# The sums of a layer norm as accumulating passes of ScalarE, and a state copy moved to GpSimd, in the first stage of a four-layer kernel

## Chip, cores and metric

One core of one Trainium2 chip. The metric is the device time of one execution in microseconds (us), on that core. All runs quoted here are of the fast state; "before" is timed again on the same chip in every set of runs, and its medians lie between 10865.7 and 10869.8 us.

The engines are named as the profile does: PE (TensorE matmul), PEld (its weight loads), DVE (VectorE), ACT (ScalarE), POOL (GpSimd), SP (the queue that issues the loads).

## The reference, cut to what matters

The model is four layers. The change touches only the first: a layer norm and two selective recurrences ("mambas") over 4 x 4096 tokens, one on the normed channels and one on the flipped ones, and a residual sum.

```python
def _layernorm(x, g, b):
    mu = jnp.mean(x, axis=-1, keepdims=True)
    var = jnp.mean(jnp.square(x - mu), axis=-1, keepdims=True)
    return (x - mu) * jax.lax.rsqrt(var + LN_EPS) * g + b
...
xs = _layernorm(x.reshape(b, -1, c), ln_g, ln_b)        # c = 192
y1 = _mamba(xs, ...)                                     # in_proj, conv, silu, x_proj, softplus,
y2 = _mamba(jnp.flip(xs, axis=-1), ...)                  # then h = dA * h + dBx, y = C . h
out = xs + y1 + y2
```

## The kernel before

It works through 32 units of 512 tokens. A unit has two recurrences of 12 quads each; a quad is four scans of 128 rows x 512 tokens on DVE, so a unit is 96 scans, 48 for each recurrence. A quad in program order:

```python
def product(self, u, k):       # DVE, or POOL for every fourth quad ("h_apart"): h = dtx * B
    engine.tensor_tensor(h, u["rows", k // 2, 1], B..., ALU.mult)
def decay(self, u, k, j):      # ACT: dA = exp(dt * A) into one of three PSUM buffers
    self.nc.scalar.activation(dA, u["rows", k // 2, 0][:, j, :], AF.Exp, scale=self.A[...])
def step(self, u, k, j):       # DVE: h = scan(dA, h), starting from the saved state
    self.nc.vector.tensor_tensor_scan(h[:, j, :], dA, h[:, j, :], self.state[...], ALU.mult, ALU.add)
def read(self, u, k):
    nc, h = self.nc, u["h", k]
    if self.shared:            # only in the first stage
        nc.scalar.copy(self.state[:, k, :], h[:, :, T - 1])
    else:
        nc.gpsimd.tensor_copy(self.state[:, k, :], h[:, :, T - 1])
    nc.gpsimd.tensor_tensor(h, h, u["C", k % 2]..., ALU.mult)   # in place, so after the copy
# sum: PE adds h up into y, which DVE then multiplies by z (the "gate", m_y in the traces);
# spread: PE writes B (PSUM), C and Bs, once per recurrence and parity of k
```

Behind these scans, all other work is dripped into the engines' queues step by step ("one step" is one scan): the norm of the next unit, its two fronts, and the output. Each is a generator; `Piece(wait=n)` holds the next piece back for n steps. The order is fixed when the program is built, and the traces here show each of DVE, ACT and POOL working through its own queue in that order (in a timeline below, ACT's dA stands behind a copy that waits 5.79 us).

```python
def front(self, xn, first, u):
    def project(e, to):
        ps = behind.bank([128, T], "ps_in")
        ...                                                      # PE: two matmuls
        return behind.later(lambda: nc.scalar.copy(to, ps))      # ACT, some steps later
    made = []
    for d in range(ND):
        yield Piece(1.7, bank=True)
        made.append(project(d, raw[:, d, K - 1 :]))              # "raw": the first projections
    ...                  # convolution, Silu, x_proj, Softplus, stores, then the same for z

def norm(u):
    ...
    for q in range(nq):                                          # nq = 4
        if q == 2:
            yield Piece(wait=1)
        nc.vector.bn_stats(stats[:, q, :], xt[:, q, :])
        nc.vector.bn_aggr(mv[:, q, :], stats[:, q, :])
    yield Piece(wait=1)
    ...                                                          # four small POOL operations: rs, shift
    yield Piece(wait=3)
    for q in range(nq):
        nc.scalar.activation(xs[:, q, :], xt[:, q, :], AF.Identity, scale=rs[...], bias=shift[...])
    ...                                                          # PE transposes, ACT copies: xT
# in the main loop, per unit:
    last = [units[n - 1]["added"]] if n else []
    behind.add(3, norm(following), Piece(wait=3, after=last))
    behind.add(1, front(following, i), Piece(after=[following["normed"]]))
```

## Time and profile before

| | before |
|---|---|
| time, median of 3 | 10868.96 us |
| first stage | about 90 to 5340 us of the span |
| one unit | 163.9 us (mean distance of the loads of x, 30 units) |
| DVE busy, 900 to 4900 us | 3891 of 4000 us |
| POOL / PE / ACT busy there | 3533 / 3287 / 2717 us |
| DVE's waits for dA, 100 to 5200 us | 62.5 + 40.0 = 102.5 us |

A busy share says how full an engine is. A bracket at the end of a timeline row says how long the engine sat idle ahead of it and who ended that. A wait is charged to the last releaser only; to see why that one was late, one has to follow it back through its own queue. This case turns on that.

### The profile page before, as it was taken

Reading aid. Unit: us, or ns where it says so; the run is one execution under the profiler, and the core shown is the slowest. Engines: PE = TensorE matmul, PEld = TensorE weight load, DVE = VectorE, ACT = ScalarE, POOL = GpSimd, SP = SyncE. Lnnn points to the kernel's source line nnn. Section 1 sums busy time; section 2 is a strip of 40 time slices with the busy share of each in tenths; the row PEclk is TensorE's granted clock in tenths of the full one; section 3 lists DMA queues with packets and bytes.
Section 4 is the critical chain, followed back from the end, with each engine's and each line's share of the span. In section 5 each row is a group of like instructions: output and inputs, shape, how many; then the busy total and the mean of one; then the engine's idle time right before and its main releaser. Section 6 shows DMA issues by size and latency. Waiting matters only on the chain. (4 is left out here: it accounts for less than half of the span.)

```text
span 10866.7 us, 97590 instructions
## 1 busy us (share of the span) xinstructions
PE 9179.8 (84%) x31352; PEld 3644.1 (34%) x31352; DVE 9098.4 (84%) x7962; ACT 6566.6 (60%) x9784; POOL 7032.3 (65%) x2688
## 2 busy tenths in 40 slices
PE   6888878888887887887679999999999987889898
PEld 2222222222322222222223333333333333455555
DVE  7999999999999999999698888888888885555552
ACT  5666666666666666666466666656666663444443
POOL 5888888888888888888666656656656661111100
PEclk7777777777777777777678889889889887999999
DMA  5666666666666666666454545445444443122110
GB/s 158 177 181 180 177 177 183 175 176 182 177 177 179 177 178 179 176 178 180 128 151 135 140 127 143 133 125 141 129 134 133 133 121 82 41 50 64 42 40 18
DMA packets 969560, 1515.13 MB, mean 139 GB/s; under 512 B 244346, under 2 KB 277150, under 8 KB 968534
## 3 DMA queue, kind: packets, MB, share of 16 engines
q1 hardware_dynamic: 968190, 1505.85, 51.4%
q8 instruction: 247, 4.05, 0.2%
q10 hardware_dynamic: 856, 3.05, 0.1%
q14 instruction: 267, 2.19, 0.1%
HBM read 1295.45 MB, written 213.12 MB: 139 GB/s over the span
## 5 line engine op out<-in xcount | busy, mean ns | idle before, releaser
L574 DVE TENSOR_TENSOR_SCAN h<-dA,m_state,h 128x512 f32<-128x512 f32 x3840 | 4668.9, 1266 | 487.4 <-ACT dA L568 422.7
L590 POOL TENSOR_TENSOR h<-h,C 128x2048 f32<-128x2048 f32 x960 | 4345.4, 4531 | 621.6 <-ACT m_state L587 480.7
L568 ACT ACTIVATE dA<-dtE,m_A 128x512 f32<-128x512 f32 x4608 | 3106.1, 687 | 1332.9 <-DVE h L574 1227.8
L561 DVE TENSOR_TENSOR h<-dtxE,B 128x2048 f32<-128x2048 f32 x960 | 2170.6, 2261 | 78.6 <-DMA dtxE<-r_dtx 65.9
L599 PE MATMUL y<-h,gather 128*32 128x512 f32 x7680 | 1281.3, 746 | 422.9 <-POOL h L590 345.2
L452 PE MATMUL ps_in<-xT,m_in_w 96*128 96x512 f32 x1536 | 939.5, 759 | 258.6 <-ACT raw L455 127.1
L1300 POOL TENSOR_TENSOR d<-d,rs 128x512 f32<-128x512 f32 x64 | 86.8, 1357 | 1589.7 <-DVE rs L1299 1569.1
L470 PE MATMUL ps_conv<-raw,m_conv 128*128 128x512 f32 x2112 | 989.3, 617 | 1.7 <-ACT xc L475 1.7
L574 DVE TENSOR_TENSOR_SCAN h_apart<-dA,m_state,h_apart 128x512 f32<-128x512 f32 x768 | 922.3, 1260 | 40.0 <-ACT dA L568 40.0
L590 POOL TENSOR_TENSOR h_apart<-h_apart,C 128x2048 f32<-128x2048 f32 x192 | 870.2, 4532 | 39.7 <-ACT m_state L587 38.0
L561 POOL TENSOR_TENSOR h_apart<-dtxE,Bs 128x2048 f32<-128x2048 f32 x192 | 889.6, 4633 | 6.0 <-ACT Bs L550 6.0
L452 PEld LDWEIGHTS ps_in<-xT,m_in_w 96*128 96x128 f32 x1536 | 351.3, 241 | 827.2 <-issue 420.5
L589 POOL COPY m_state<-h 128x4 f32<-128x4 f32 x384 | 72.3, 188 | 849.5 <-DVE h L574 813.5
L470 PEld LDWEIGHTS ps_conv<-raw,m_conv 128*128 128x128 f32 x2112 | 417.9, 202 | 599.0 <-issue 562.4
L1049 PE MATMUL ps_dw<-strip,dw 96*96 96x512 f32 x1152 | 578.7, 650 | 1.3 <-ACT x L1058 0.9
L599 PEld LDWEIGHTS y<-h,gather 128*32 128x32 f32 x7680 | 164.7, 117 | 1225.4 <-POOL h L590 552.0
L506 POOL TENSOR_TENSOR raw<-dt,xc 128x1536 f32<-128x1536 f32 x96 | 330.0, 3437 | 294.6 <-ACT dt L505 294.6
L486 PE MATMUL ps_x<-xc,m_pack 128*44 128x512 f32 x576 | 351.0, 758 | 199.5 <-ACT xc L482 194.6
L1465 PE MATMUL sed_ps<-xn,sed 64*128 64x256 f32 (+3 forms) x2944 | 485.9, 404 | 7.0 <-DVE y L1484 7.0
L568 ACT ACT_TABLE_LOAD x345 | 442.6, 1283 | 28.5 <-DMA dtE<-r_dt 22.3
L452 PE MATMUL ps_in<-xn,m_in_w 96*128 96x512 f32 x768 | 399.0, 666 | 47.4 <-ACT z L455 31.2
L378 PE MATMUL ps_o<-hid,t 128*96 128x512 f32 x768 | 390.4, 647 | 34.3 <-ACT hid L371 13.0
(193 smaller groups left out, 12217.1 us busy)
## 6 DMA issues: line engine op xcount, KB each, us to landing
dtE<-r_dt SPq DMA_DIRECT2D x2304, 256.0 KB, 5.0
dtxE<-r_dtx SPq DMA_DIRECT2D x2304, 256.0 KB, 4.1
r_dt<-dt SPq DMA_DIRECT2D x96, 768.0 KB, 4.0
r_dtx<-raw SPq DMA_DIRECT2D x96, 768.0 KB, 5.4
x<-x SPq DMA_DIRECT2D x64, 384.0 KB, 3.9
img<-x SPq DMA_DIRECT2D x28, 512.0 KB, 8.2
xt<-in_x SPq DMA_DIRECT2D x32, 384.0 KB, 5.8
x<-o SPq DMA_DIRECT2D x32, 384.0 KB, 5.0
```

What stands on the lines that cost most here:

```text
L378: nc.tensor.matmul(ps, self.w2[:, m, bass.ts(k, CP)], h[:, m, :], start=(m == 0), stop=(m == NH - 1),)
L452: nc.tensor.matmul(ps, self.in_w[:, k, bass.ts(e, 128)], xn[:, k, :], start=(k == 0), stop=(k == 1))
L470: nc.tensor.matmul(ps, self.conv[:, d, j, :], raw[:, d, j : j + T], start=(j == 0), stop=(j == K - 1))
L486: nc.tensor.matmul(ps, self.x_w[:, d, :], xc[:, d, :], start=(d == 0), stop=(d == ND - 1))
L506: nc.gpsimd.tensor_tensor(dtx, dt, xc, ALU.mult)
L561: engine.tensor_tensor(h, u["rows", k // 2, 1], u[B, k % 2].unsqueeze(1).broadcast_to([128, 4, T]), ALU.mult)
L568: self.nc.scalar.activation(dA, u["rows", k // 2, 0][:, j, :], AF.Exp, scale=self.A[:, k, j : j + 1])
L574: self.nc.vector.tensor_tensor_scan(h[:, j, :], u.pop(("dA", k, j)), h[:, j, :], self.state[:, k, j : j + 1], ALU.mult, ALU.add,)
L590: nc.gpsimd.tensor_tensor(h, h, u["C", k % 2].unsqueeze(1).broadcast_to([128, 4, T]), ALU.mult)
L599: self.nc.tensor.matmul(u["ys"][32 * j : 32 * j + 32, :], self.ex.gather[:, i // 2, :], h[:, j, :], start=(i == 0), stop=(i == 3 and not s ...
L1049: nc.tensor.matmul(ps, dw[:, k, j, :], s[:, k, dy : dy + rows, dx : dx + HW], start=(j == 0), stop=(j == 8),)
L1465: nc.tensor.matmul(out, sed[p, int(h is not None), i ^ position(k, s), cols], xn[b, g][p, c, :], start=group(t) not in begun, stop=left[gr ...
```

## The change

The intent: DVE is the fullest engine of the stage, so take the norm's statistics off it. ACT makes the two sums in passes with an accumulator output, and loses the state copies, which POOL does itself ahead of its product.

```diff
     def read(self, u, k):
-        if self.shared:
-            nc.scalar.copy(self.state[:, k, :], h[:, :, T - 1])
-        else:
-            nc.gpsimd.tensor_copy(self.state[:, k, :], h[:, :, T - 1])
+        nc.gpsimd.tensor_copy(self.state[:, k, :], h[:, :, T - 1])
 ...
         def norm(u):
-            for q in range(nq):
-                if q == 2:
-                    yield Piece(wait=1)
-                nc.vector.bn_stats(stats[:, q, :], xt[:, q, :])
-                nc.vector.bn_aggr(mv[:, q, :], stats[:, q, :])
-            yield Piece(wait=1)
-            (POOL: rs = (var + EPS) ** -0.5; shift = -mean * rs)
+            def sums(func, to, **args):
+                for q in range(nq):
+                    if q:
+                        yield Piece(wait=1)
+                    nc.scalar.activation(xs[:, q, :], xt[:, q, :], func, accum_out=to[:, q : q + 1], ...)
+            yield from sums(AF.Identity, shift)
+            yield Piece(wait=2)
+            nc.gpsimd.tensor_scalar(shift, shift, -1.0 / C, None, ALU.mult)
+            yield Piece(wait=2)
+            yield from sums(AF.Square, rs, bias=shift)
+            yield Piece(wait=2)
+            (POOL: rs = (rs / C + EPS) ** -0.5; shift = shift * rs)
             yield Piece(wait=3)
             (the last pass, unchanged)
```

The chain of the norm gets longer: in the built order its last transposed copy moves from scan 33 of a unit to scan 43.

More of the change, by code (lines that the diff above doesn't have):

```diff
@@ L776, in norm @@
             xt = u["x"]
-            stats = work.tile([128, nq, 6], F32, name="stats")
-            mv = work.tile([128, nq, 2], F32, name="mv")
-            rs = work.tile([128, nq], F32, name="rs")
-            for q in range(nq):
-                if q == 2:
-                    yield Piece(wait=1)
-                nc.vector.bn_stats(stats[:, q, :], xt[:, q, :])
-                nc.vector.bn_aggr(mv[:, q, :], stats[:, q, :])
-            yield Piece(wait=1)
-            shift = work.tile([128, nq], F32, name="shift")
-            nc.gpsimd.tensor_scalar(rs, mv[:, :, 1], EPS, None, ALU.add)
+            shift, rs = (work.tile([128, nq], F32, name=n) for n in ("shift", "rs"))
+            xs = work.tile([128, nq, C], F32, name="xs", bufs=1)
+            def sums(func, to, **args):
+                for q in range(nq):
+                    if q:
+                        yield Piece(wait=1)
+                    nc.scalar.activation(
+                        xs[:, q, :], xt[:, q, :], func, accum_out=to[:, q : q + 1],
+                        **{n: v[:, q : q + 1] for n, v in args.items()},
+                    )
+            yield from sums(AF.Identity, shift)
[4 more added lines that the diff above has]
+            yield Piece(wait=2)
+            nc.gpsimd.tensor_scalar(rs, rs, 1.0 / C, EPS, ALU.mult, ALU.add)
             nc.gpsimd.tensor_tensor(rs, rs, minus_half, ALU.pow)
-            nc.gpsimd.tensor_tensor(shift, mv[:, :, 0], rs, ALU.mult)
-            nc.gpsimd.tensor_scalar(shift, shift, -1.0, None, ALU.mult)
+            nc.gpsimd.tensor_tensor(shift, shift, rs, ALU.mult)
             yield Piece(wait=3)
-            xs = work.tile([128, nq, C], F32, name="xs", bufs=1)
             for q in range(nq):
```

## The prediction

> **What bounds the kernel now.** I read the page first, then a table of engine time by stretch, the groups of instructions by shape and the waits inside the first stage, and last the timeline of one unit there. The change touches only the first stage (the later stages never take the removed branch), which the busy tenths show as the first 19 or 20 of 40 slices: VectorE (DVE) stands at 9 there and no other engine does.
>
> ```profile
> DVE  7999999999999999999698888888888885555552
> ACT  5666666666666666666466666656666663444443
> POOL 5888888888888888888666656656656661111100
> PEclk7777777777777777777678889889889887999999
> ```
>
> The table by stretch (columns: length, then busy us of PE, weight load, DVE, ACT, POOL, then granted clock, DMA share, GB/s) gives the sizes in 800 us of the stage:
>
> ```profile
> 2500.00:3300.00 800.00, 657.44 (x2034) 226.01 (x2038) 777.85 (x628) 546.37 (x882) 706.99 (x199) 0.77 0.65 178
> ```
>
> DVE 97%, GpSimd (POOL) 88%, PE 82%, ScalarE (ACT) 68%. So the stage is a DVE stream with small holes, and POOL is the next candidate. Rows by shape, for the window 100 to 5200 us (31 of the stage's 32 units of 512 tokens):
>
> ```profile
> L574 DVE TENSOR_TENSOR_SCAN h<-dA,m_state,h 128x512 f32<-128x512 f32 x2240 | 2706.8, 1265 | 99.9 <-ACT dA L568 62.5 <-DVE h L561 1.8
> L590 POOL TENSOR_TENSOR h<-h,C 128x2048 f32<-128x2048 f32 x561 | 2537.8, 4532 | 575.4 <-ACT m_state L587 468.8 <-issue 54.5 <-DMA dtE<-r_dt 34.3
> L574 DVE TENSOR_TENSOR_SCAN h_apart<-dA,m_state,h_apart 128x512 f32<-128x512 f32 x747 | 897.2, 1260 | 40.0 <-ACT dA L568 40.0
> L590 POOL TENSOR_TENSOR h_apart<-h_apart,C 128x2048 f32<-128x2048 f32 x186 | 843.1, 4533 | 39.1 <-ACT m_state L587 37.4
> L587 ACT COPY m_state<-h 128x4 f32<-128x4 f32 x560 | 106.4, 190 | 111.6 <-DVE h L574 109.3
> L794 ACT ACTIVATE xs<-xt,shift,rs 128x192 f32<-128x192 f32 x124 | 60.7, 537 | 25.2 <-POOL shift L790 25.2
> L783 DVE BATCH_NORM_STATS2 stats<-xt 128x6 f32<-128x192 f32 x124 | 41.0, 331 | 0.0
> L784 DVE BATCH_NORM_AGGREGATE mv<-stats 128x2 f32<-128x6 f32 x124 | 22.6, 182 | 4.3
> ```
>
> To be seen: the norm's 124 + 124 statistics stand on the bounding engine, 63.6 us in all; DVE's named holes are 62.5 + 40.0 us of waiting for dA, ACT's decay factors; and POOL spends 468.8 us waiting for ACT's copy of the last state, which is really waiting for DVE's scan with ACT in between.
>
> The DVE timeline shows what the statistics cost in place:
>
> ```profile
> 2754.31 1.28 DVE L574 TENSOR_TENSOR_SCAN h<-dA,m_state,h 128x512 f32<-128x512 f32 x1 [0.24 <-ACT dA L568]
> 2755.51 0.34 DVE L783 BATCH_NORM_STATS2 stats<-xt 128x6 f32<-128x192 f32 x1
> ...
> 2756.44 1.25 DVE L574 TENSOR_TENSOR_SCAN h<-dA,m_state,h 128x512 f32<-128x512 f32 x1
> 2757.61 0.33 DVE L783 BATCH_NORM_STATS2 stats<-xt 128x6 f32<-128x192 f32 x1
> ...
> 2758.53 2.42 DVE L574 TENSOR_TENSOR_SCAN h<-dA,m_state,h 128x512 f32<-128x512 f32 x2
> ```
>
> Between the scans they take 2756.44 - 2755.51 = 0.93 and 2758.53 - 2757.61 = 0.92 us: 1.85 us a unit, a little less than 4 x (331 + 182) = 2.05 because neighbours overlap. The same place one unit earlier is at 2591.68, so a unit lasts 2755.51 - 2591.68 = 163.8 us.
>
> **What the Trainium skill says.** (1) "ScalarE: Activation LUTs", section "What ACT_TABLE_LOAD costs": an ACTIVATE with immediate operands takes 186 ns + 0.833 ns per element, each per-partition pointer adds about 93, neighbours overlap by about 93. The trace agrees: 128x192 with two pointers should be 186 + 160 + 186 = 532 ns, the row has 537. (2) "ScalarE activation tables: per-element evaluation and per-set limits", section "What a function is on this engine", says that the accumulator output adds the results along the free dimension and works whatever the table; it gives no price for reading it out, and the trace has no ACTIVATE with one. That is my largest unknown. (3) "SBUF — State Buffer", section "Who interferes with whom": a DVE instruction with at most one SBUF input does not contend with GpSimd. DVE's scans and products here take one operand from PSUM; POOL's product is 4532 ns in one group and 4533 in the other, whatever runs beside it, so I expect no new contention from POOL's copies. No page names bn_stats.
>
> **The change part by part.**
>
> Statistics off DVE: 8 instructions a unit go, worth 1.85 us on the path. Over 31 units that follow the first: 57 us. This is the firm part.
>
> Sums onto ACT: 4 Identity passes without pointers, 186 + 160 = 346 ns, and 4 Square passes with one, 439 ns (estimates from the page above): 4 x 346 + 4 x 439 = 3.1 us a unit, plus the reading of the accumulator, which I guess at 0 to 0.25 us each, so 3.1 to 5.1. Away from ACT go 24 copies x 190 = 4.6 us. ACT's total stays about level, at 68%. No table is reloaded: the built program has 783 loads in both.
>
> Copies onto POOL: 24 a unit. The second stage already does this:
>
> ```profile
> L589 POOL COPY m_state<-h 128x4 f32<-128x4 f32 x384 | 72.3, 188 | 849.5 <-DVE h L574 813.5
> ```
>
> 24 x 188 = 4.5 us a unit. POOL had 88% of 163.8 = 145 us of work, now about 150 of some 161 us, 93%: still under the bound. In return it need not wait for ACT. Where ACT is in a table burst this matters: at the unit above DVE finished a quad at 2588.0 and POOL began its product only at 2591.47 because ACT's copy sat behind a Silu with two table loads.
>
> Order: in the built program the norm's first passes stand 23 scans into a unit (statistics before: 21), and the last transposed copy moves from scan 33 to 43. The Silu and Softplus that end the next front stay at scans 66 and 79 (67 and 79 before) and the stores at 80 and 84 as before: the ten scans of delay come out of slack. PE gets the same work in a shorter stretch.
>
> Now the burst, walked by hand with the trace's durations. Without statistics DVE reaches the quad after them 1.85 us earlier. There DVE has two waits for dA, 0.49 and 0.31 us, around the Softplus with its two table loads, and then 0.45 and 0.74 us around the Silu of z. The new passes lie just there: two Squares before Softplus, and the third between Softplus and the next dA. I get dA ready about 0.3 us after DVE wants it after Softplus, and 0.45 and 0.7 us around Silu: one wait of about 0.5 us goes, the rest stays. With the state copies gone from ACT, another 0.1 to 0.2 us at the other table bursts (0.87 and 0.29 us of wait) goes. A slow accumulator adds 3 x 0.25 = 0.75 us to the Softplus wait and takes this back. Net 0.6 us gained a unit, between -0.5 and +1: 31 x 0.6 = 19 us.
>
> Start: DVE's weight preparation begins 1.8 us earlier without the four statistics in front, and its loads and stores set the first scan; 2 us. Sum: 57 + 19 + 2 = 78 us, 10869 - 78 = 10791 us.
>
> **The rivals.** (a) The saving is swallowed by ACT. ACT now waits twice a unit for POOL (the mean's sign and scale, then rs and shift), and POOL runs its queue in order behind products of 4.5 us. In my walk the first hand-over is just in time (POOL done at 2602.45, ACT there at 2602.4) and the second makes ACT wait about 3 us, while DVE has two decays in hand, about 2.4 us of scans plus a product of 2.26. A slip of a few us there would stop DVE. For it: ACT already waited 25.2 us for shift. Against: the longest of those was 0.9 us, and POOL is ahead of its old place by 3 us. If 2 us a unit were lost, the time would be about 10850. (b) POOL becomes the bound: at 93% a backlog would hold the h buffers and DVE's product would wait. Against: that product has no wait at all today, and POOL's idle time is over 500 us in the stage. If it came true, 10860 to 10900. (c) Earlier POOL products and a freer ACT remove all of DVE's waits: 31 x (1.85 + 3.3) = 160 us, 10709. Against: the waits come from bursts of 4 us on ACT, which stay.
>
> **Range and chances.** The centre leans on the firm 57 us plus a small part of the waits: I say 10793. Low 10745 is 57 us plus two thirds of the 102 us of waits; high 10850 is rival (a). Faster by over 2% would need 217 us, more than (c) has: 1%. Slower by over 2% needs 7 us lost in every unit: 1%.
>
> **What would show it.** DVE's groups of statistics gone, its stage about 77 us shorter with the scans still at 1265 ns; its waits for dA near 80 to 100 us in all instead of 102; POOL's waits named DVE, not ACT, its copies near 188 ns and its busy share 92 to 93%; the Identity sums near 350 ns and the Squares near 440. I am wrong if the passes last over 700 ns, if ACT waits for POOL's shift for over 4 us a unit with DVE's waits growing alongside, or if DVE's product begins to wait for POOL or PE.

## The result, and the profile after

| | before | after |
|---|---|---|
| median, 4 runs each | 10869.77 us | 10865.05 us |
| ratio after / before | | 0.9996, 95% interval 0.9978 to 1.0013 |
| one unit | 163.92 us | 163.92 us |
| DVE's waits for dA, 100 to 5200 us | 102.5 us | 167.6 us |
| first scan of the stage starts at | 93.80 us | 90.22 us |

The time is the same, 72 us above the forecast of 10793 us and 15 us above its high end. (A ratio is the mean time of one kernel's fast runs over that of the other's in the same rounds, so it is not quite the ratio of the medians quoted.) The 4 us that are left are the earlier start of the first scan; a unit did not get shorter at all.

The busy tenths after: DVE as full as it was, POOL now also at 9.

```profile
DVE  7999999999999999999698888888888885555552
POOL 6999999999999999999666656656656661111100
```

The row of the same 800 us of the stage (PE, PEld, DVE, ACT, POOL, clock, DMA, GB/s): DVE's busy time is down by 11 us and POOL's is up by 18.

```profile
2500.00:3300.00 800.00, 646.14 (x2032) 224.62 (x2033) 766.88 (x588) 549.91 (x845) 724.76 (x315) 0.80 0.66 177
```

The groups after, for the same 5100 us (busy, mean ns, then the idle time before them and who ended it):

```profile
L574 DVE TENSOR_TENSOR_SCAN h<-dA,m_state,h 128x512 f32<-128x512 f32 x2238 | 2698.4, 1264 | 201.4 <-ACT dA L568 164.5 <-DVE h L561 1.8
L574 DVE TENSOR_TENSOR_SCAN h_apart<-dA,m_state,h_apart 128x512 f32<-128x512 f32 x748 | 894.3, 1257 | 3.1 <-ACT dA L568 3.1
L586 POOL COPY m_state<-h 128x4 f32<-128x4 f32 x560 | 106.3, 190 | 390.5 <-DVE h L574 329.1 <-ACT Bs L550 45.2 <-PE ps_conv L470 11.6
L797 ACT ACTIVATE xs<-xt,shift,rs 128x192 f32<-128x192 f32 x124 | 60.9, 539 | 78.1 <-POOL shift L794 78.1
L781 ACT ACTIVATE xs<-xt,shift 128x192 f32<-128x192 f32 x124 | 54.9, 443 | 8.3 <-POOL shift L788 8.3
L781 ACT ACTIVATE xs<-xt 128x192 f32<-128x192 f32 x122 | 43.4, 355 | 0.0
L781 ACT ACTIVATION_READ_ACCUMULATOR xs<-xt 128x1 f32 x122 | 23.2, 191 | 0.0
```

The statistics are gone and the new instructions cost what was estimated. But the scans' waits for dA rose by 164.5 + 3.1 - 102.5 = 65 us, about the 63.6 us of the statistics. That the two cancel so exactly is chance: the experiments below move either without the other.

**Where the waits are.** I sorted DVE's bracketed waits of all units by the time since that unit's own load of x was issued, in bins of 6 us. Sums over the stage, bins under 3 us not counted:

| us into the unit | before | after | what runs there |
|---|---|---|---|
| 54 to 84 | 60.2 | 40.5 | Softplus and Silu of z of the second front, with table loads on ACT |
| 90 to 102 | none | 112.3 | DVE changes from the first recurrence to the second; raw projections of the next front |

So there is a new hole, in one place. The timeline of the changed kernel there (rows between are left out, as in the later timelines):

```profile
2633.12 6.66 PE L452 MATMUL ps_in<-xT,m_in_w 96*128 96x512 f32 x8
2636.94 0.59 ACT L455 COPY raw<-ps_in 128x512 f32<-128x512 f32 x1 [5.79 <-PE ps_in L452]
2637.42 0.70 ACT L568 ACTIVATE dA<-dtE,m_A 128x512 f32<-128x512 f32 x1
2638.15 1.28 DVE L574 TENSOR_TENSOR_SCAN h<-dA,m_state,h 128x512 f32<-128x512 f32 x1 [2.30 <-ACT dA L568]
2639.81 0.59 ACT L455 COPY raw<-ps_in 128x512 f32<-128x512 f32 x1 [1.69 <-PE ps_in L452]
2641.03 1.28 DVE L574 TENSOR_TENSOR_SCAN h<-dA,m_state,h 128x512 f32<-128x512 f32 x1 [1.59 <-ACT dA L568]
```

Read from the bottom: DVE waits for dA; the dA ahead of it in ACT's queue is a copy of a raw projection; that copy waits 5.79 us for PE; and PE is only then at these matmuls. DVE loses 2.30 + 1.59 = 3.89 us in this unit. Before, the same projections stood in a quieter stretch (raw copies at scans 41 to 44 of a unit, now 48 to 50) and PE took 3.60 us for as many of them:

```profile
2624.58 3.60 PE L452 MATMUL ps_in<-xT,m_in_w 96*128 96x512 f32 x8
2629.98 1.98 PE L452 MATMUL ps_in<-xT,m_in_w 96*128 96x512 f32 x4 [1.80 <-ACT raw L455]
```

PE's granted clock differs too, as the table by stretch (columns as above) shows, first of the kernel before, then of the changed one:

```profile
2624.00:2630.00 6.00, 4.20 (x11) 1.54 (x9) 5.26 (x5) 5.96 (x8) 5.94 (x4) 1.00 1.03 267
```

```profile
2630.00:2636.00 6.00, 6.00 (x14) 1.53 (x13) 5.75 (x4) 1.15 (x2) 5.86 (x5) 0.50 0.65 169
```

"TensorE: Matmul & The Clock Gate" of the Trainium skill, Part 1, says that the default state is throttled and that activity releases it. The low clock here, 0.50, begins at 2622.0 us, 1.7 us after the end of an idle gap of PE of 3.18 us, so the trace does not contradict it, but no run here sets the clock. A trace below shows that the half clock alone does not make the hole; whether the hole needs it stays open.

### The profile page after: what moved, and what is told of

Its sections match the earlier page's. It is cut to its first block, busy times and chain, and to the rows that moved or that the text cites. A ratio compares the mean times of both kernels' runs of the same rounds, so it can differ in the third digit from the quotient of the medians.

```text
span 10862.8 us, 98460 instructions
## 1 busy us (share of the span) xinstructions
PE 9068.7 (83%) x31352; PEld 3627.0 (33%) x31352; DVE 9036.3 (83%) x7706; ACT 6584.5 (61%) x9528; POOL 7168.9 (66%) x3456
## 5 line engine op out<-in xcount | busy, mean ns | idle before, releaser
L596 PE MATMUL y<-h,gather 128*32 128x512 f32 x7680 | 1226.6, 715 | 434.8 <-POOL h L587 271.8
L452 PE MATMUL ps_in<-xT,m_in_w 96*128 96x512 f32 x1536 | 1049.5, 836 | 288.1 <-ACT z L455 258.5
L586 POOL COPY m_state<-h 128x4 f32<-128x4 f32 x960 | 181.2, 189 | 1283.4 <-DVE h L574 1179.1
L574 DVE TENSOR_TENSOR_SCAN h_apart<-dA,m_state,h_apart 128x512 f32<-128x512 f32 x768 | 918.2, 1257 | 3.1 <-ACT dA L568 3.1
L587 POOL TENSOR_TENSOR h_apart<-h_apart,C 128x2048 f32<-128x2048 f32 x192 | 868.1, 4521 | 15.5
L452 PEld LDWEIGHTS ps_in<-xT,m_in_w 96*128 96x128 f32 x1536 | 382.1, 266 | 984.4 <-issue 448.9
```

The source lines that it names most:

```text
L452: nc.tensor.matmul(ps, self.in_w[:, k, bass.ts(e, 128)], xn[:, k, :], start=(k == 0), stop=(k == 1))
L574: self.nc.vector.tensor_tensor_scan(h[:, j, :], u.pop(("dA", k, j)), h[:, j, :], self.state[:, k, j : j + 1], ALU.mult, ALU.add,)
L587: nc.gpsimd.tensor_tensor(h, h, u["C", k % 2].unsqueeze(1).broadcast_to([128, 4, T]), ALU.mult)
L596: self.nc.tensor.matmul(u["ys"][32 * j : 32 * j + 32, :], self.ex.gather[:, i // 2, :], h[:, j, :], start=(i == 0), stop=(i == 3 and not s ...
```

## The experiments

Three theories after the result. **P (place):** the longer norm pushes the next front's first projections onto the changeover between the recurrences, where PE is behind, and ACT's in-order queue carries that to DVE. **Rivals:** Q, the accumulating passes fill ACT; R, the copies on POOL (now 91% busy) make the sums of y late, and so PE. Twelve kernels ran; all gave correct results but the two meant to be wrong.

| run | norm | statistics | state copies | median us | ratio to before | DVE waits for dA, us |
|---|---|---|---|---|---|---|
| e1 delay only | late | DVE | ACT | 10900.50 | 1.0030 | 144.3 |
| e2 copies only | old place | DVE | POOL | 10831.14 | 0.9966 | 71.8 |
| e3 sums only | late | ACT | ACT | 10966.52 | 1.0092 | 264.9 |
| e4 early sums | early | ACT | POOL | 10761.83 | 0.9903 | 67.2 |
| e5 no statistics | old place | none | ACT | 10870.32 | 1.0000 | 159.6 |
| e6 front held | late, front later still | ACT | POOL | 10762.03 | 0.9901 | 68.4 |
| e7 raw copies later | late | ACT | POOL | 10867.24 | 0.9998 | 95.2 |
| e8 early sums, scan 4 | early | ACT | POOL | 10727.55 | 0.9868 | 33.8 |
| e9 no statistics, copies | old place | none | POOL | 10764.02 | 0.9906 | 66.8 |
| e10 early statistics, copies | early | DVE | POOL | 10776.61 | 0.9918 | 25.2 |
| e11 early sums | early | ACT | ACT | 10731.08 | 0.9873 | 39.5 |
| e12 delay and held front | late, front later still | DVE | ACT | 10768.11 | 0.9910 | 19.4 |

Medians of before in the same sets: 10867.29 (e1 to e4), 10869.43 (e5 to e8), 10865.73 us (e9 to e12).

**e1, the delay by itself**, in the kernel before:

```diff
-            yield Piece(wait=3)
+            yield Piece(wait=13)
             xs = work.tile([128, nq, C], F32, name="xs", bufs=1)
```

> The kernel before with one edit: the norm waits ten steps more before its last pass, so its transposes and the next front's first projections stand where the changed kernel has them (built order: raw copies at scans 48 and 50 of a unit, 41 to 44 before). Statistics stay on DVE, state copies on ACT. Theory P (place): ACT stops at the copies of the projections behind PE, DVE's waits for dA grow by 2 to 4 us a unit over the 102 us of the kernel before, time 10930 to 10990 us. Rival Q (the accumulating passes fill ACT) and rival R (the copies on POOL make the sums of y and so PE late): neither edit is in here, so 10870 +- 15 us.

```profile
ACT raw L455 <- PE ps_in L452: 231.3, 93, 5.6
```

It is 33 us slower, clear of noise (1.0018 to 1.0041). The hole is there without any of the new instructions: 123.5 us in the bins from 90 to 102 us, and ACT's wait for the raw projections grows from 76.7 to 231.3 us (the line above: total, times, longest). The size I expected was too large, for a reason I had not seen: the waits between 54 and 84 us, 60.2 us before, are all but gone. The norm's last pass no longer stands between the table loads there, which is likely why; no run tests it alone. P holds for the hole at the changeover; Q and R cannot explain it, as neither edit is in.

**e2, the copies alone** (only the `read` part of the change), and **e3, the sums alone** (the change with `read` as before):

> The kernel before with the state copies on POOL alone; statistics on DVE, order of the norm as before. P: no hole at the changeover, DVE's waits 60 to 102 us, 10840 to 10870 us. Q: the same. R: PE late behind POOL, DVE's waits over 150 us, 10900 us or more.

> The changed kernel with the state copies back on ACT; sums on ACT, norm late as in the changed kernel. P: the hole is there, DVE's waits 150 to 220 us, 10865 to 10910 us. Q: the same. R: no hole, about 10800 us.

The copies alone gain 36 us, 9 us more than the best that was expected; the sums alone lose 99 us, more than any theory said. 36 and -99 do not add up to the change's 4: with ACT's copies back, POOL waits for ACT and ACT waits for POOL. In e3, ACT waits 67.5 us for the first shift and 70.8 us for the second (8.3 and 78.1 in the changed kernel), and DVE's waits between 54 and 66 us of a unit are 88 us, beside 138 us at the changeover. R is out: with the copies off POOL the hole at the changeover stands.

**e4, the same passes earlier.** Only the writing of xT has to wait for the unit before, so the sums need not:

```diff
-behind.add(3, norm(following), Piece(wait=3, after=last))
+behind.add(3, norm(following, last), Piece(wait=8))
 ...
-            yield Piece(wait=3)
+            yield Piece(wait=3, after=list(last))          # ahead of the last pass
```

> The changed kernel with the same passes and copies, but the sums start at scan 8 of the unit, not 23, and only the last pass waits for the unit before to be written; the next front's projections are back at their old place (raw copies at 41 to 44). P: the hole of 3.9 us a unit is gone and the saving appears, DVE's waits at or under 100 us, 10750 to 10810 us. Q and R: same passes, same copies, so 10850 to 10870 us.

As P said: 10761.83 us, and nothing in the bins from 90 to 102. Q is out for this hole: the passes are the same here, and in e1 the hole came without them.

**e5, the statistics taken out** of the kernel before (wrong result on purpose; `mv` is a constant tile), to weigh the term that the prediction called firm:

```diff
-                nc.vector.bn_stats(stats[:, q, :], xt[:, q, :])
-                nc.vector.bn_aggr(mv[:, q, :], stats[:, q, :])
```

> Wrong result on purpose: the kernel before without its eight statistics instructions per unit (mean and variance are a constant tile of ones); all else in its old order. Theory F (the statistics stand on the path, 1.85 us a unit as the prediction had it): 10800 to 10820 us, DVE's waits still about 100 us. Rival S (they only fill time in which DVE would wait for ACT): waits grow to 150 us or more and 10850 to 10870 us.

It gains nothing. The time is that of before to within 0.1%, and the holes between 54 and 60 us grow from 15.8 to 68.5 us. The timeline of this kernel:

```profile
2584.22 4.81 DVE L574 TENSOR_TENSOR_SCAN h<-dA,m_state,h 128x512 f32<-128x512 f32 x4
2586.66 1.28 ACT L482 ACT_TABLE_LOAD   x1
2592.21 0.18 ACT L587 COPY m_state<-h 128x4 f32<-128x4 f32 x1
2592.47 4.55 POOL L590 TENSOR_TENSOR h<-h,C 128x2048 f32<-128x2048 f32 x1 [5.62 <-ACT m_state L587]
2596.95 4.68 POOL L561 TENSOR_TENSOR h_apart<-dtxE,Bs 128x2048 f32<-128x2048 f32 x1
2603.43 0.24 POOL L789 TENSOR_SCALAR shift<-shift 128x4 f32<-128x4 f32 x1
2603.70 0.98 ACT L793 ACTIVATE xs<-xt,shift,rs 128x192 f32<-128x192 f32 x2 [2.72 <-POOL shift L789]
2605.37 1.28 DVE L574 TENSOR_TENSOR_SCAN h_apart<-dA,m_state,h_apart 128x512 f32<-128x512 f32 x1 [1.58 <-ACT dA L568]
```

Here is a second chain: a Silu with a table load on either side holds up ACT's copy of the state (only the first load is shown); POOL can't begin its product until it is made (5.62 us idle, of which 3.4 us lie after the end of the quad's last scan at 2589.03); two POOL products of over 4.5 us follow; then the norm's shift; ACT waits for it; dA is late; DVE waits. DVE's statistics are not in this chain. Without them DVE only reaches its wait sooner.

**e6, the front held back** until after the changeover, in the changed kernel, and **e7, ACT's copies of the raw projections three steps later**, there too:

```diff
-behind.add(1, front(following, i), Piece(after=[following["normed"]]))
+behind.add(1, front(following, i), Piece(wait=0 if i else 15, after=[following["normed"]]))   # e6
```

```diff
-made.append(project(d, raw[:, d, K - 1 :]))
+made.append(project(d, raw[:, d, K - 1 :], 3 if self.shared else 0))     # e7: steps more until the copy
...                                    # (cut: project and later hand the number on)
```

> The changed kernel, norm as late as there, but the next front starts later still, after the changeover between the two recurrences (raw copies at scans 55 to 57 of a unit, 48 to 50 in the changed kernel). P, sharpened to the collision of these projections with the changeover's spreads of B and C: the hole 90 to 100 us into each unit (112 us in all in the changed kernel) goes, DVE's waits 50 to 70 us, 10745 to 10790 us. If a late norm costs wherever its front lies: waits stay over 130 us, 10840 us or more.

> The changed kernel with ACT's copies of the raw projections issued three steps later in ACT's order, the matmuls almost at their old place. If the link is ACT standing in order behind PE: ACT's waits for these projections fall from 256 us to under 120, the hole shrinks by half or more, 10780 to 10830 us. If PE's lateness reaches DVE by another way (B's spread before DVE's product): hole and time stay, 10850 us or more.

e6 did as expected: no hole at the changeover, 103 us faster than the changed kernel, by one number. It also tells about the clock. Here are the same 18 us of a unit, from 78 to 96 us after the load of x, in the changed kernel and then in e6 (columns as in the table by stretch):

```profile
2622.00:2640.00 18.00, 17.17 (x31) 5.19 (x26) 15.03 (x12) 9.02 (x16) 14.71 (x9) 0.53 0.50 130
2734.00:2752.00 18.00, 16.20 (x33) 4.42 (x30) 17.90 (x15) 11.57 (x19) 16.13 (x9) 0.50 0.50 133
```

The granted clock is 0.53 and 0.50, but DVE is busy for 15.03 us in the one and 17.90 in the other. So the half clock alone does not make the hole.

e7 is a miss in its time. The link is as stated (ACT's wait for the projections falls from 256.2 to 46.2 us, and the bins from 90 to 102 us are empty), but new waits come up elsewhere: 72.8 us on DVE's gate, which waits for PE's y right after the changeover, and 29.5 us at the first Silu of the second front, 42 to 48 us into the unit. So getting ACT out of PE's way is not enough. PE is still late there, at a mean clock of 0.51 from 78 to 102 us into the unit; PSUM banks held longer may add to it, which I did not test.

```profile
DVE h L574 <- ACT dA L568: 74.8, 124, 3.8
DVE m_y L619 <- PE y L606: 72.8, 29, 2.6
```

**e8, the early sums four scans earlier** (`wait=4` instead of 8):

> As the early sums, four scans earlier (scan 4): the last pass stands at 23 to 24 instead of 24 to 26, fronts at the same place. A search for a better place only: within 15 us of the 10762 us of the early sums, holes at the Softplus burst smaller by some us; if the first sum meets a load that has not landed, 10 to 30 us slower.

10727.55 us, better than the bounds I gave. The last pass at scans 23 and 24 leaves the Softplus burst alone: the waits between 54 and 84 us fall from 37.7 us in e4 to 5.1. DVE is busy 3951 of 4000 us.

```profile
DVE h L574 <- ACT dA L568: 20.2, 17, 4.6
DVE h_apart L574 <- ACT dA L568: 13.6, 21, 1.1
```

**e9 to e12, closing the account.** e9 is e5 with the copies on POOL; e10 is e8 with statistics on DVE; e11 is e8 with the copies on ACT; e12 is e1 with e6's line.

> Wrong result on purpose: without the statistics (constants instead), and with the state copies on POOL; everything else in its old order. The run without statistics but with the copies on ACT gained nothing, its hole near 54 us of a unit grew by 53 us while ACT's wait for POOL's shift grew from 25 to 81 us. Theory H (POOL, held up by ACT's copies behind the table loads, hands the shift over late, and that sets the pace there): with the copies gone from ACT the statistics' 1.85 us a unit do appear: 10831 - 57, so 10765 to 10785 us, ACT's wait for shift under 30 us. Rival (the statistics never cost DVE anything): 10825 to 10835 us.

> Statistics on DVE, copies on POOL, the norm's first half at scans 5 to 7 and its last pass at 23, as in the best kernel so far. Under H and P the order is clean, so what is left between this and the 10727 us of the early sums on ACT is the 1.85 us a unit of the statistics: 10775 to 10795 us. If the place alone made the gain and the sums give nothing: 10725 to 10740 us.

> The best kernel so far (sums from scan 4) with the state copies back on ACT. If the copies matter only where the norm's hand-overs cross a table burst: 10730 to 10750 us. If they cost the 36 us of the run with the copies alone: 10755 to 10775 us, with DVE's waits up by as much.

> Statistics on DVE and copies on ACT as before; only two places change: the norm ten scans later, the next front held until after the changeover (raw copies at scans 55 to 57). P: against the delay alone (10900 us) the hole of 123 us 90 to 100 us into each unit goes, and the holes of 60 us that the delay had removed stay away: 10775 to 10810 us, with not one instruction taken from DVE. If place is not the cause: 10865 us or more.

e9 (10764.02 us, 1 us better than the range expected): with the copies off ACT, taking the statistics away gains 10831.14 - 10764.02 = 67 us (the two are of different sets, whose before differs by 1.6 us), and ACT's wait for the shift, 81.2 us in e5, is gone from the list of waits, as it is in e2. So the same eight instructions a unit are worth nothing with the copies on ACT and 67 us with them on POOL. e10: the order and the copies, with statistics on DVE, bring 89 us; moving the sums to ACT on top of it (e8) brings 49 us by the medians and 54 by the ratios, near the 57 us of the prediction's first term. e11: in the clean order the copies are worth nothing that can be told from noise (3.5 us; one of its four runs was at 10716 us). e12: 98 us gained with no instruction moved to another engine, by two numbers in the order, and 7 us better than the range expected. Of DVE's 62.5 us of waits ahead of the scans of h, 14.0 are left:

```profile
DVE h L574 <- ACT dA L568: 14.0, 18, 4.9
```

## Why the prediction was wrong

- **"The ten scans of delay come out of slack. PE gets the same work in a shorter stretch": this step failed, and it is what cost the gain in the changed kernel.** I checked that Silu, Softplus and stores at the end of the front kept their places, and did not look at what the front's first projections now met. They met the changeover, 112 us of waits (e1, e4, e6, e12 show that place is the cause). My hand walk ended at the scan after the Silu, 14 us short of it (2621.6 and 2635.9 us in the changed kernel's timeline). With the front held past the changeover and nothing else changed, the kernel gains 103 us (e6), more than the 78 us of the sum.
- **"Statistics off DVE ... worth 1.85 us on the path ... This is the firm part": wrong as argued, though it did not decide the result.** The 1.85 us were time on DVE, not time on the path. e5 shows that in the kernel before they are covered by a chain over a Silu's table loads on ACT, ACT's state copy, POOL's products and the shift. They are worth about their size where that chain is cut (e9, 67 us; e10 to e8, 49 us). The changed kernel moves the copies too and so takes ACT's copy out of that chain; the prediction did not see that the term hangs on this. So far as the term held, it was luck. I called the term firm because DVE was 97% busy; a fullest engine with named waits is not yet a bound at each place.
- **The walk through the burst was right as far as it went.** I gave 0.3, 0.45 and 0.7 us for the waits around Softplus and Silu; the trace of the same unit has 0.29, 0.29 and 0.74. ACT's wait at the second hand-over was put at about 3 us and is 78.1 / 30 = 2.6.
- **The costs of the instructions were right:** Identity 355 ns for 346 forecast, Square 443 for 439, the accumulator 0.19 us for a guess of 0 to 0.25, POOL's copies 190 ns, POOL at 91% for 92 to 93. No new contention showed: with 768 more copies on POOL its products stayed at 4521 to 4534 ns and DVE's scans at 1257 to 1264, as taken from "SBUF — State Buffer", section "Who interferes with whom" (its sentence also excepts DVE's 2-port modes, which the prediction left out).
- **The start** was put at 2 us and gave 3.6.
- **Copies:** I counted 0.1 to 0.2 us a unit for them beside the bursts. Alone they gave 36 us, 1.2 us a unit (e2): the 25 us of waits from 54 to 66 us into the unit, where the chain of e5 ends, are gone, and 20 us at the unit's start, while about 20 us came up from 66 to 90. I had seen that POOL's product began 3 us late because of ACT's copy, and did not follow it on to the shift and to dA.
- **Rivals:** (a), ACT swallowing the gain, came nearest, but by its wait for PE, not for POOL; the wait for POOL's shift is what hit e3. (b) did not come: DVE's product never waited for POOL or PE in the changed kernel.

What stays open: whether the hole at the changeover would also come with PE at full clock; e6 shows only that the half clock without the projections there does not make it. And in e11 one run was 15 us faster than the other three; the rest do not say why.

## What to carry to other kernels

Before moving work off the fullest engine, follow each of its waits back through the queues of the engines that release it; work that stands next to such a wait may be free already, as in e5, and its removal then only lengthens the wait. A change that lengthens a side chain also moves everything that the chain starts: look at what those instructions now stand beside, in the queues of all engines, not only at whether the chain's end still meets its date. In a kernel whose order is set by hand, a change of places without any change of instructions (e12, 98 us) can be worth more than the change of engine, and the two should be tested apart.

## What the Trainium skill lacked or had wrong

- "ScalarE: Activation LUTs", section "What ACT_TABLE_LOAD costs": its price of an ACTIVATE fits (355 and 443 ns measured, 346 and 439 by its rule), but it does not say that an accumulator output brings an instruction of its own: ACTIVATION_READ_ACCUMULATOR, 187 to 191 ns each here.
- The prediction says that no page names bn_stats. Two pages name batch-norm statistics as an operation of DVE, but none that I found prices bn_stats and bn_aggr: 331 ns for 128x192 f32 and 182 ns for the aggregate, 0.46 us the pair in place.
- "GPSIMD Engine Reference": I found no figure there for very small operations. Here a copy of 128x4 took 190 ns and a power (ALU pow) of 128x4 f32 1037 ns.
